# A six-stage decoder kernel: where the products with ones and the division stand in the causal attentions' order

## Chip, cores, metric

The kernel runs on one core of a Trainium2 chip. The metric is the device time of one execution in microseconds, from the first to the last instruction with what lies around them; smaller is better. Times of runs are given as a median with the lowest and highest. A profile is one execution, taken by the hardware profiler.

The engines are named as in the profile: PE is TensorE (PEld its weight loads), DVE VectorE, ACT ScalarE, POOL GpSimd, SP the engine that issues most DMAs. Each runs its own instructions in the order of the program and waits for the others by semaphores.

## What is computed

A decoder of two layers over 8 batches of 256 tokens with 512 features, all in float32. Six stages follow one another, each with its residual and layer norm. Three of them are causal attentions, and the change lies in what these share:

```python
x = _layernorm(x + _L0_attn_ref(x, ...))     # differential attention: 32 query heads of 16
x = _layernorm(x + _L0_xattn_ref(x, ...))    # long convolution
x = _layernorm(x + _L0_ffn_ref(x, ...))      # 8 experts, top 2
x = _layernorm(x + _L1_attn_ref(x, ...))     # self attention: 16 heads of 32
x = _layernorm(x + _L1_xattn_ref(x, ...))    # cross attention
x = _layernorm(x + _L1_ffn_ref(x, ...))      # routed attention: 16 heads, shared keys and values
```

In each of the three, for queries q, keys k and values v of a head:

```python
scores = jnp.einsum('bhqd,bhkd->bhqk', q, k) * scale
scores = jnp.where(causal, scores, ...)
probs = jax.nn.softmax(scores, axis=-1)
out = jnp.einsum('bhqk,bhkd->bhqd', probs, v)
```

The differential attention then takes every second head's output, times a factor lambda, from its neighbour's, and normalizes each head's row by the root of its mean square.

## The kernel before, in words

`causal_attention` is one function, called three times: named "a" (the differential one, 8 units a batch, with a function `gather`), "s" (self attention, 4 units a batch) and "r" (routed, 4 units a batch). A *unit* is four heads of one batch of 256 tokens. There are 64 units in "a" and 32 in each of the others. Units are worked on in *slots*: slot u does the first step for unit u, the second for an earlier unit, the third for one still earlier. With `upb` units a batch, the second step is `wait = upb + 1` slots behind and the third `lag = upb + 2`.

The steps of a unit:

- `maxima(u)`: 12 score products (L1287) into `ps_sc`, a group of four PSUM banks with one buffer only. ScalarE copies them to SBUF (`rows`, L1296; two buffers, in "s" one), GpSimd masks them (L1298), VectorE takes the maxima of the rows (L1307), at the slot's end. At the end of a batch VectorE splits these maxima into three bfloat16 terms (`split`, L1314 to L1321), and in the next slot TensorE turns them (`turn`, L1329).
- `weights(u)`: the scores again, transposed, less the maxima (L1350, L1359), into the same `ps_sc` buffer, so after the copy L1296. ScalarE takes the exponential into `pT` (L1367), which frees `ps_sc` for the next slot's maxima. GpSimd masks it (L1368) and, except in the last batch, adds two of its blocks (L1378), so that the sums below need half the products.
- `products(u)`: weights times values (L1393) into one half of the PSUM tile `ps_pv` (one buffer, in the last batch two), weights times ones (L1403) into the other half. VectorE takes the reciprocal of the sums (L1411), then the quotient: in "s" and "r" by one multiplication (L1417), in "a" by `gather`. The products with values need the mask L1368, those with ones the sum L1378 as well.

`gather` in "a" multiplies by the reciprocal for units of even number in the batch (L438). For odd ones VectorE also multiplies by minus lambda (`second`, L441), and GpSimd adds that to the even one's (L442), in `yT`.

Around these, slots do other work of TensorE, in order of due time: projections for later groups, transposes, output projections (`fill`, by a budget; `need`, what is due). What is to happen later is noted by `at(slots, place, ...)`: at a slot's "start", at its "mid", at its "end", or as work to "fill". `add_norm_later` adds an output to x; GpSimd's reciprocal root (L145, L146) is issued at that slot's "end", and the norm is applied at the next slot's "mid" by VectorE (L160).

`finish` runs after the last unit of a batch. In "a" it notes, among others, ScalarE's Square of all of `yT` at the next slot's "start" (L562), so ahead of that slot's copy L1296 in ScalarE's order, then sums of squares on TensorE (L514) and VectorE's means (L521). In "s" and "r" the output work of the batch is filled in from the next slot on. "s" has at "mid" also VectorE's sums of arriving tokens (L1214), and "r" the spreading of keys (L2145) before they are transposed (L2069).

The order on TensorE, VectorE, ScalarE and GpSimd is the order of the program (`manual_schedule`). A slot before the end of the units runs: maxima, some fill, `sums(u)` (products, with reciprocal and division, and at the end of a batch `finish`), the events at "mid", `weights`, more fill, what is due, the turn, a last fill, the rows' maxima, the events at "end". In the last slots, where no new unit begins, `weights` stand first and `sums` behind them.

## Time and profile before

| | us |
|---|---|
| runs: median (lowest to highest), 3 runs | 2091.62 (2087.61 to 2092.78) |
| profiled execution | 2084.03 |
| its span, first to last instruction | 2082.3 |
| TensorE busy | 1926.0 |
| VectorE busy | 1236.9 |
| GpSimd busy | 851.9 |
| ScalarE busy | 615.3 |
| mean granted TensorE clock | 0.979 |

Busy time of the engines in stretches that lie within the three attentions:

| attention | stretch, us | PE | DVE | ACT | POOL |
|---|---|---|---|---|---|
| "a" | 52 to 445 (393) | 352.30 | 286.69 | 213.43 | 280.83 |
| "s" | 1140 to 1435 (295) | 290.15 | 180.85 | 116.71 | 136.18 |
| "r" | 1880 to 2036 (156) | 136.50 | 131.55 | 82.01 | 105.43 |

How to read the profile: an instruction is given with its line, its engine, what it writes and reads, and the tile's shape. An engine's idle time stands before the instruction that ended it, with what released that instruction. Matmuls overlap, so their busy time is that of the union. One row of the order of time can stand for several instructions alike. Each float32 product appears as two matmuls. An instruction can have waited for several others; the one that came last is named.

Slots are numbered from 0 in each attention and begin with the maxima's first product. In "a" slot 0 begins at 14.62 us and slot 63 at 388.91; in "s" slot 0 at 1101.90; in "r" slot 0 at 1826.90.

### The profile page before, as it was taken

To read this page: it belongs to the slowest core of one execution; us is meant where nothing else is said; L and a number is where in the kernel's file an instruction comes from. 1 tells how busy PE (TensorE), PEld (TensorE's weight loads), DVE (VectorE), ACT (ScalarE), POOL (GpSimd) and SP (SyncE) were. 2 spreads that over 40 slices of the span, in tenths; PEclk is the share of its full clock that TensorE was granted. 3 is DMA by queue.
4 is the path that set the end of the run, shared out by engine and by line. 5 is a ranking of instruction groups with operands and counts; after the bars stand their busy time and mean duration, and the time that the engine had idled before them with its cause. 6 is when DMAs were issued, how large, how long until landed. Compare 5 with 4: busy or idle time off the path is not lost. (4 is left out here: it accounts for less than half of the span.)

```text
span 2082.3 us, 46237 instructions
## 1 busy us (share of the span) xinstructions
PE 1926.0 (92%) x20068; PEld 1122.6 (54%) x20068; DVE 1236.9 (59%) x1879; ACT 615.3 (30%) x787; POOL 851.9 (41%) x945
## 2 busy tenths in 40 slices
PE   7979999879999999999969999998999999988985
PEld 5545555444444446666635545544878778454443
DVE  4677777658889876122225657457343442536887
ACT  4555555520000003211114344431101011235552
POOL 2677777646555834000014545344000000216763
PEclk9999999989999999999989999999999999999997
DMA  6799943326114217223122202002000000170000
GB/s 220 307 399 387 386 139 78 88 69 224 44 58 140 80 51 233 85 72 138 61 86 83 78 31 89 3 2 103 21 21 31 21 31 1 43 233 12 30 24 31
DMA packets 141627, 220.27 MB, mean 106 GB/s; under 512 B 27440, under 2 KB 56240, under 8 KB 141424
## 3 DMA queue, kind: packets, MB, share of 16 engines
q1 hardware_dynamic: 134960, 196.97, 27.5%
q0 software_dynamic: 6464, 20.32, 2.9%
q8 instruction: 160, 2.62, 0.5%
q14 instruction: 43, 0.35, 0.1%
HBM read 106.51 MB, written 123.34 MB: 110 GB/s over the span
## 5 line engine op out<-in xcount | busy, mean ns | idle before, releaser
L1411 DVE RECIPROCAL rsum<-ps_pv 128x256 f32<-128x256 f32 x128 | 224.5, 1754 | 220.2 <-PE ps_pv L1403 220.2
L177 PE MATMUL ps_y<-kv,wt 128*128 128x512 f32 x640 | 280.2, 597 | 5.4 <-POOL kv L607 2.7
L1367 ACT ACTIVATE pT<-ps_k 128x1536 f32<-128x1536 f32 x128 | 185.7, 1451 | 239.1 <-PE ps_k L1359 233.5
L1307 DVE TENSOR_REDUCE neg<-rows 128x12 f32<-128x1536 f32 x128 | 222.9, 1742 | 48.2 <-POOL rows L1298 48.1
L1296 ACT COPY rows<-ps_q 128x1536 f32<-128x1536 f32 x128 | 184.1, 1438 | 154.2 <-PE ps_q L1287 101.1
L1368 POOL TENSOR_SCALAR_AFFINE_SELECT pT<-pT 128x1024 f32<-128x1024 f32 x128 | 140.7, 1100 | 186.2 <-ACT pT L1367 186.1
L177 PEld LDWEIGHTS ps_y<-kv,wt 128*128 128x128 f32 x640 | 120.9, 191 | 156.7 <-issue 137.4
L1298 POOL TENSOR_SCALAR_AFFINE_SELECT rows<-rows 128x1024 f32<-128x1024 f32 x128 | 141.2, 1103 | 154.0 <-ACT rows L1296 153.4
L1378 POOL TENSOR_TENSOR pT<-pT 128x512 f32<-128x512 f32 x112 | 147.1, 1313 | 9.3
L1204 POOL DMA_INDIRECT w_l1x<-ys,slots x32 | 33.5, 1046 | 258.5 <-DMA ys<-y_m 250.9
L207 PE MATMUL ps_f<-xT,w_l1a 128*32 128x256 f32 x2048 | 122.0, 384 | 0.7 <-ACT xT L232 0.7
L145 POOL TENSOR_SCALAR rstd<-bn_mv 128x1 f32<-128x1 f32 x80 | 16.6, 207 | 206.8 <-DVE bn_mv L151 200.5
L1112 PE MATMUL po_m<-dn,hT 128*128 (+1 forms) x216 | 98.7, 594 | 1.0 <-ACT hT L1102 1.0
L1403 PE MATMUL ps_pv<-pT,ones_v 128*32 128x256 f32 (+1 forms) x1152 | 85.2, 378 | 14.7 <-POOL pT L1378 14.6
L645 DVE TENSOR_REDUCE yc<-z 128x64 f32<-128x512 f32 x128 | 86.2, 674 | 5.6 <-POOL w_l1a L646 5.2
L207 PEld LDWEIGHTS ps_f<-xT,w_l1a 128*32 128x32 f32 x2048 | 62.2, 111 | 45.3 <-issue 7.3
L1287 PE MATMUL ps_q<-kz,qT 32*128 32x128 f32 x1536 | 62.2, 292 | 16.8 <-ACT pT L1367 13.4
L1287 PEld LDWEIGHTS ps_q<-kT,qT 32*128 32x128 f32 x1536 | 48.7, 186 | 50.4 <-ACT pT L1367 17.3
L1350 PE MATMUL ps_k<-qT,kT 32*128 32x256 f32 (+1 forms) x1024 | 69.8, 359 | 5.1 <-ACT rows L1296 2.9
L1287 PEld LDWEIGHTS ps_q<-kz,qT 32*128 32x128 f32 x1536 | 49.8, 190 | 45.4 <-ACT pT L1367 31.8
L1091 DVE TENSOR_TENSOR h_b<-h_b,pg 128x352 f32<-128x352 f32 x36 | 18.8, 521 | 92.4 <-ACT h_b L1090 92.4
L1287 PE MATMUL ps_q<-kT,qT 32*128 32x128 f32 x1536 | 61.0, 288 | 13.4 <-ACT pT L1367 8.5
(385 smaller groups left out, 3617.4 us busy)
## 6 DMA issues: line engine op xcount, KB each, us to landing
xs<-zero SPq DMA_DIRECT2D x8, 4352.0 KB, 32.5
ys<-zero SPq DMA_DIRECT2D x8, 4352.0 KB, 33.1
filters<-in_L_xattn_k SPq DMA_DIRECT2D x4, 2560.0 KB
first_h<-xs SPq DMA_DIRECT2D x36, 256.0 KB, 2.7
ys<-y_m SPq DMA_DIRECT2D x36, 256.0 KB, 2.0
gu<-in_L_ffn_gate_up_proj SPq DMA_DIRECT2D x3, 2816.0 KB, 16.4
wt<-filters SPq DMA_DIRECT2D x32, 256.0 KB, 2.6
sorted_x<-zero SPq DMA_DIRECT2D x1, 5120.0 KB, 34.7
```

The lines of the kernel that those rows point to most:

```text
L177: nc.tensor.matmul(ps, lhsT=lhsT(k), rhs=rhs(k), start=(k == 0), stop=(k == n - 1))
L207: nc.tensor.matmul(ps[cs], lhsT=lhsT[:, cs], rhs=rhs, start=start, stop=stop)
L645: nc.vector.tensor_reduce(yc[:, lb], z, AX.X, ALU.add)
L1112: nc.tensor.matmul(po, lhsT=hT[:m, i, :], rhs=dn[i][:m, bass.ds(e, 1), :], start=(i == 0), stop=(i == len(FCH) - 1),)
L1287: nc.tensor.matmul(block[:, s, j, :], lhsT=q(rows, c, b * S + i * P, P), rhs=k(rows, c, b * S + keys * P, P), start=True, stop=True,)
L1296: nc.scalar.copy(d.rearrange("p j s k -> p s j k"), block)
L1298: nc.gpsimd.affine_select(out=rows, in_=rows, compare_op=ALU.is_ge, fill=-FAR, base=0, pattern=[[0, 8], [-1, P]], channel_multiplier=1,)
L1307: return lambda: nc.vector.tensor_reduce(neg[u // upb % 2][:, :, :, c], d, AX.X, ALU.max, negate=True)
L1367: nc.scalar.activation(p[:, 0:3].rearrange("p j s q -> p s j q"), block, AF.Exp)
L1368: nc.gpsimd.affine_select(out=p[:, 0:2].rearrange("p j s q -> p (j s) q"), in_=p[:, 0:2].rearrange("p j s q -> p (j s) q"), compare_op=ALU ...
L1378: nc.gpsimd.tensor_tensor(p[:, 3], p[:, 1], p[:, 2], ALU.add)
L1411: nc.vector.reciprocal(r, ps[:, 1, :])
```

## The change

`products(u)` is cut in two. Its first part allocates the PSUM tile and issues the products with the values. It returns a function, `divided`, that issues the rest: the products with ones, the reciprocal, and the division or `gather`. `sums(u)` returns a function too, which calls `divided` and, at the end of a batch, `finish`. In the slots that begin a unit that function is called behind the events at "mid" and behind `weights`; in the last slots it is called at once.

On TensorE the products with ones thus stand behind the scores for the weights. On VectorE the reciprocal and the division stand behind what is issued at "mid". On GpSimd the addition L442 of `gather` stands behind the mask L1368 and the sum L1378 that `weights` issue. What `finish` notes is noted behind them, for the same later slots. No instruction is added or left out.

```diff
+                def divided():
+                    first = p[:, 0:3:2] if late else p[:, 0:4:3]
+                    for j in range(2 if late else 1):
+                        for s in range(4):
+                            nc.tensor.matmul(
+                                ps[32 * s : 32 * s + 32, 1, j * P :],
+                                lhsT=ones_v,
+                                rhs=p[:, 1, s, :] if j else first[:, :, s, :],
...
+                    r = work.tile([P, S], F32, tag="rsum", name="rsum")
+                    nc.vector.reciprocal(r, ps[:, 1, :])
...
+                return divided
...
             def sums(u):
-                nonlocal per_batch
-                if lag <= u < units + lag:
-                    products(u - lag)
+                if not lag <= u < units + lag:
+                    return lambda: None
+                divided = products(u - lag)
+
+                def rest():
+                    nonlocal per_batch
+                    divided()
                     if (u - lag) % upb == upb - 1:
                         n = (u - lag) // upb
                         per_batch = finish(work, pools, 2 * n, yT.pop(n), at)
+
+                return rest
...
-                    sums(u)
+                    rest = sums(u)
                     happen("mid")
                     if u >= wait:
                         weights(u - wait)
+                    rest()
...
-                    sums(u)
+                    sums(u)()
```

More of the change, by code (lines that the diff above doesn't have):

```diff
@@ L1399, in products @@
                         )
-                first = p[:, 0:3:2] if late else p[:, 0:4:3]
-                for j in range(2 if late else 1):
-                    for s in range(4):
-                        nc.tensor.matmul(
-                            ps[32 * s : 32 * s + 32, 1, j * P :],
-                            lhsT=ones_v,
-                            rhs=p[:, 1, s, :] if j else first[:, :, s, :],
-                            start=(j == 0),
-                            stop=(j == 1 or not late),
-                        )
-                r = work.tile([P, S], F32, tag="rsum", name="rsum")
-                nc.vector.reciprocal(r, ps[:, 1, :])
-                if c == 0:
-                    yT[u // upb] = work.tile([P, KB, S], F32, tag="yT", name="yT_b")
-                if gather:
-                    gather(work, pools, at, yT[u // upb], u // upb, c, ps[:, 0, :], r)
-                else:
-                    nc.vector.tensor_tensor(yT[u // upb][:, c, :], ps[:, 0, :], r, ALU.mult)
+                def divided():
[6 more added lines that the diff above has]
+                                rhs=p[:, 1, s, :] if j else first[:, :, s, :],
+                                start=(j == 0),
+                                stop=(j == 1 or not late),
+                            )
+                    r = work.tile([P, S], F32, tag="rsum", name="rsum")
+                    nc.vector.reciprocal(r, ps[:, 1, :])
+                    if c == 0:
+                        yT[u // upb] = work.tile([P, KB, S], F32, tag="yT", name="yT_b")
+                    if gather:
+                        gather(work, pools, at, yT[u // upb], u // upb, c, ps[:, 0, :], r)
+                    else:
+                        nc.vector.tensor_tensor(yT[u // upb][:, c, :], ps[:, 0, :], r, ALU.mult)
+                return divided
             upg = 2 * upb
```

## The prediction

> **What bounds the kernel now.** I read the table of busy time first, then TensorE's waits over the whole span, then the same waits inside the first attention, then one pair of slots in order of time.

> ```profile
> PE 1926.0 (92%) x20068; PEld 1122.6 (54%) x20068; DVE 1236.9 (59%) x1879; ACT 615.3 (30%) x787; POOL 851.9 (41%) x945
> ```

> TensorE (PE) is busy 92% of the span. Only its idle time, or work of it that other waits hide, can be won. The waits (who, line, waited for: us in total, times, longest) that touch the change:

> ```profile
> PE ps_q L1287 <- ACT pT L1367: 21.9, 18, 1.6
> PE ps_pv L1403 <- POOL pT L1378: 14.6, 34, 0.6
> ...
> PE ps_k L1350 <- ACT rows L1296: 3.8, 10, 0.7
> ```

> and, of these, in the first attention alone (0 to 450 us):

> ```profile
> PE ps_q L1287 <- ACT pT L1367: 13.4, 12, 1.6
> PE ps_pv L1403 <- POOL pT L1378: 11.1, 26, 0.6
> ```

> So the products with ones wait for GpSimd's sum L1378, and the next maxima wait for the exponential L1367 to free the one score buffer. Those two are what the change can win. The scores for the weights hardly wait for the copy L1296 now: 3.8 us. Slots 33 and 34 of the first attention in order of time (start, length, engine, line):

> ```profile
> 198.49 0.95 PE L1287 MATMUL ps_q<-kz,qT 32*128 32x128 f32 x24
> ...
> 199.51 1.44 ACT L1296 COPY rows<-ps_q 128x1536 f32<-128x1536 f32 x1 [1.23 <-PE ps_q L1287]
> ...
> 200.26 0.83 PE L1393 MATMUL ps_pv<-pT,v 128*32 128x256 f32 x16
> ...
> 200.91 0.61 PE L1403 MATMUL ps_pv<-pT,ones_v 128*32 128x256 f32 x8
> ...
> 201.45 0.71 PE L1350 MATMUL ps_k<-qT,kz 32*128 32x256 f32 x8
> 201.59 1.76 DVE L1411 RECIPROCAL rsum<-ps_pv 128x256 f32<-128x256 f32 x1 [0.75 <-PE ps_pv L1403]
> ...
> 202.68 1.45 ACT L1367 ACTIVATE pT<-ps_k 128x1536 f32<-128x1536 f32 x1 [1.73 <-PE ps_k L1359]
> ...
> 203.95 0.73 POOL L442 TENSOR_TENSOR yT_b<-yT_b,second 128x256 f32<-128x256 f32 x1 [1.84 <-DVE quads L505]
> 204.18 0.76 PEld L1287 LDWEIGHTS ps_q<-kz,qT 32*128 32x128 f32 x24 [0.68 <-ACT pT L1367]
> ...
> 204.63 1.09 POOL L1368 TENSOR_SCALAR_AFFINE_SELECT pT<-pT 128x1024 f32<-128x1024 f32 x1
> 204.71 1.06 ACT L562 ACTIVATE w_l<-yT_b 128x1024 f32<-128x1024 f32 x1 [0.58 <-POOL yT_b L442]
> ...
> 205.68 1.42 ACT L1296 COPY rows<-ps_q 128x1536 f32<-128x1536 f32 x1
> ...
> 205.81 1.28 POOL L1378 TENSOR_TENSOR pT<-pT 128x512 f32<-128x512 f32 x1
> ...
> 207.71 0.71 PE L1350 MATMUL ps_k<-qT,kz 32*128 32x256 f32 x8
> ```

> Two distances set a slot. From the maxima to the scores for the weights at least 0.95 + 0.07 + 1.44 + 0.05 = 2.51 us (maxima, handover, copy, handover). From those scores to the next maxima at least 1.10 + 0.12 + 1.45 + 0.05 = 2.72 us (the score group is 1.10 long). Slot 33 has 2.96 and 2.73. Also to be seen: L442 runs ahead of L1368 on GpSimd, which so starts at 204.63 though the exponential ended at 204.13; and the Square L562 stands on ScalarE ahead of slot 34's copy.

> **The change, part by part.** *Eight products with ones move* behind the scores. They last 0.61 us and overlap the product before them by 0.18, so they are worth 0.43. In slot 33 the first distance falls from 2.96 to 2.53, just above 2.51, and the second takes the 0.43: a slot without waits gains nothing. The cover of the copy is gone: what is late on ScalarE in front of it is now late on TensorE.

> *Slots that wait.* Where L1403 waits for the sum (22 times in the inner slots of the first attention), the first distance falls to the 2.51 floor: slot 14, for example, has 2.40 + 0.95 = 3.35, so 3.35 - 2.51 - 0.43 = 0.41. With 0.40 each, 8.8 us. Where the next maxima wait for the exponential, the moved 0.43 hides in that wait; seven such slots away from the heads' turn treated below: 3.0 us. Three slots (29, 35, 59) already stand at the copy's floor and only get the ones added: -1.3 us. Sum: 10.5 us won, of 24.5 waited. Bounds: 0 to 24.5; the floors decide for the middle.

> *GpSimd's order.* In the first attention L442 now stands behind L1368 and L1378 (it was ahead). That helps the sum, and is in the 0.40 above. But once in eight slots the Square reads what L442 wrote, and the next copy stands behind the Square. Slot 33 and 34 anew: scores at 201.02; exponential 202.25 to 203.70; L1368 to 204.84; L1378 from 204.93 to 206.21; L442 to 206.95; Square from 207.00, copy 0.97 behind its start, as now, from 207.97 to 209.39; scores at 209.44, where now they are at 207.71: +1.73, and the ones behind them +0.43, together 2.2 us. The reciprocal is not what is late: 202.73 + 1.76 + 0.03 + 0.49 = 205.01, before 206.2. This happens in slots 18, 26, 34, 42, 50 and 58. By the same working slot 26, where VectorE is late anyhow, pays 1.1, and slot 50, whose forerunner wins nothing, 2.7. Six times 2.2 is +13.2 us (bounds 6.6 and 16.2).

> *VectorE's order.* Reciprocal and division start 1.10 + 0.61 - 0.43 less the old overlap, about 1.15 us, later; the rows' maxima L1307 queue behind them, at the end of a batch the split into terms, and behind that TensorE's turn L1329. In the order of time the turn follows its terms by 0.96, 0.46, 0.90, 0.65, 3.62 and 0.26 us in the first attention's inner turns. VectorE's small copies there took 0.97 to 1.18 us instead of 0.20 where a GpSimd instruction was running, so part of the shift is met by such a pause falling away. I take 2.0 us over three turns (none: 0; the whole shift at five: 5.8). The end of the first and third attention hangs on such a turn (waits 0.79 and 1.92 us): +1.1 each.

> [...]

> *Second attention.* Its TensorE is busy 290.15 of 295 us (1140 to 1435). No waits for the sum. Two slots at the copy's floor: +0.9. Three copies were late because VectorE finished the maxima late (TensorE waits 0.34, 0.68, 0.34); VectorE's norms and sums at "mid" now run in the time in which it waited for the ones, so some two thirds of 1.36 go: -0.9. Net 0.

> *Third attention.* Won: slot 7 of it 0.7 (its products waited 1.47 for the mask, the ones 0.50 for the sum); keys spread at "mid" now stand ahead of the reciprocal, so the waits of 0.65, 1.07 and 1.07 for L2145 shrink, less what the turn behind takes back: 1.55; two exponential waits 0.8. Lost: twice VectorE's two norms (1.95 us for both) stand ahead of the reciprocal where the next product waits for its buffer: 0.7 each; the tail 1.1. Net -0.5.

> No DMA, no instruction is added or removed. SP's queue is passed only at "mid", whose output stores stay where they were, before the scores.

> The switch between groups of 32*128 and 128*32: each costs the overlap of 0.18 less 0.07, 0.11 us. Filled slots have as many as before; ten empty ones get two more, 2.2 us, inside the exponential's wait of up to 1.6: taken at nothing, 2.2 if uncovered. [...]

> **Sum.** First attention -10.5 + 13.2 + 2.0 + 1.1 = +5.8; second 0; third -0.5. Together +5.3 us on the profiled execution, 2084.03 us (span 2082.3 and 1.7 around it): 2089.3. That execution lies 7.6 below the median of the runs, 2091.62, so on their scale I forecast 2097 us.

> **Rivals.** *The late L442 is cheap.* If the Square or the copy behind it is not what slots 18 to 58 wait for, 13.2 goes and the wins stay: -8 us, 2084. For it: 24.5 us of waits lie open. Against: ScalarE's row for L562 shows it starting with L442's end and the copy with its own. Chance 0.17.

> *VectorE's shift is paid everywhere.* In the third attention VectorE is busy 131.55 of 156 us (1880 to 2036). If there the division's end, not TensorE, lets the next product in, from the point where its slack (in quiet slots the next product starts 2.75 us after the reciprocal ends, 0.42 of it the division) is under the 1.15 shift plus the norms that now stand ahead, each of some 12 slots pays 1.0: 2097 + 12 = 2109. Against: quiet slots keep over 1 us. Chance 0.16.

> *The change does nothing to the order,* because TensorE's weight loads run ahead or the balance is exact: 2091.6. The order is written by hand on four engines, so I give 0.05. The forecast keeps 0.62.

> **How the numbers follow.** The forecast's own range is 2092 to 2103 (the bounds 6.6 and 16.2 of the Square, 0 and 5.8 of the turns). With part of both rivals: 2085 to 2107. A measurement here tells 0.3%, 6.3 us: 2085.3 and 2097.9. The forecast lies inside that, with some 0.47 of its weight above 2097.9: slower 0.62 x 0.47 + 0.16 = 0.45; same 0.62 x 0.53 + 0.05 = 0.38; faster 0.17.

> **What would show it.** Right: L1403 no longer waits for L1378; L1350 waits for L1296 far more than 3.8 us, most of it in six places behind L562; L562 waits for L442 over a microsecond where now it is at most 0.6; L1378 ends before L442 starts; L1287's wait for L1367 falls below 21.9. Wrong: if waits for L1296 stay near 4 us, the Square was no matter, and the kernel is faster; if L1393 comes to wait for L1417 or L438 in many slots, VectorE's shift is the cause and the time lies above 2103.

## The result, and the profile after

| | before | after |
|---|---|---|
| runs: median (lowest to highest), us | 2090.57 (2087.61 to 2092.78) | 2116.45 (2116.31 to 2125.73) |
| ratio of times, with its 95% interval | | 1.0138 (1.0120 to 1.0155) |
| profiled execution, us | 2084.03 | 2116.31 |
| its span, us | 2082.3 | 2114.6 |
| mean granted TensorE clock | 0.979 | 0.972 |

The changed kernel is 1.4% slower. The forecast was 2097 us, with a range up to 2107. Slower had the largest of the three chances; the size lay outside the range.

In the changed kernel the product with ones is L1404, the reciprocal L1412, the division L1418; the lines up to L1393 keep their numbers. From the page, the table of busy time and two of the costliest groups (busy time and mean ns of one, idle time before them and its releaser):

```profile
PE 1939.1 (92%) x20068; PEld 1134.9 (54%) x20068; DVE 1227.1 (58%) x1879; ACT 618.4 (29%) x787; POOL 847.6 (40%) x945
...
L1404 PE MATMUL ps_pv<-pT,ones_v 128*32 128x256 f32 (+1 forms) x1152 | 89.3, 393 | 0.0
L1350 PE MATMUL ps_k<-qT,kz 32*128 32x256 f32 (+1 forms) x1024 | 71.0, 364 | 19.6 <-ACT rows L1296 19.3
```

TensorE does the same 20068 products and is busy 13 us longer, at a mean clock of 0.972 in place of 0.979. The products with ones no longer wait for anything (0.0, before 14.7). The scores for the weights now wait for the rows' copy. TensorE's waits over the whole span (us in total, times, longest):

```profile
PE ps_k L1350 <- ACT rows L1296: 26.6, 32, 3.4
...
PE ps_q L1287 <- ACT pT L1367: 11.8, 15, 1.1
PE ps_pv L1393 <- POOL pT L1368: 10.8, 8, 2.8
PE ps_n L1329 <- DVE terms L1318: 8.6, 5, 3.0
PE ps_pv L1393 <- DVE yT_b L1418: 7.6, 6, 2.7
PE ps_ss L514 <- ACT w_l L562: 6.4, 2, 3.4
PE ps_pv L1393 <- POOL rows L1298: 6.2, 2, 3.1
PE pt_ss L527 <- DVE means L521: 5.0, 5, 2.0
...
PE ps_o L207 <- DVE yT_b L559: 4.4, 3, 2.2
...
PE ps_n L1329 <- DVE yT_b L559: 3.2, 1, 3.2
```

L1350's wait went from 3.8 to 26.6 us, L1287's from 21.9 to 11.8, and the 14.6 of L1403 are gone. So both announced wins are there, and the announced loss is larger than both. New in size are L1393's wait for the division L1418 (before 2.7), L514's for the Square (2.5), and L207's and L1329's for VectorE's scaling L559 (0.9 each). The two waits that the profile puts down to GpSimd's mask of the rows, L1298, belong to the division as well: these products don't read the rows, and in both places (slots 116 and 124) the division ended 0.03 to 0.05 us before that mask.

Where the 32.3 us of the two spans lie, worked out from the first product of each slot's maxima in the two traces (from start to start; the first attention up to the start of slot 63):

```
part                                              before    after   difference
before slot 0 of the first attention               14.62    13.66     -1.0
first attention: slots 18, 26, 34, 42, 50, 58      42.18    63.92    +21.7
first attention: slots that became shorter                          -10.9
first attention: other slots that became longer                      +9.9
between first and second attention                712.99   715.62     +2.6
second attention, slot 0 to 31                    295.44   295.37     -0.1
up to slot 1 of the third                         437.44   438.01     +0.6
third attention, slot 1 to 31                     201.15   210.12     +9.0
behind                                             46.39    46.80     +0.4
```

The stretch between the first and the second attention begins with the first attention's slot 63, which has the new order, and its last slots; the long convolution and the experts behind them have no changed code. Its 2.6 us have no explanation here: in the kernels below, some on other chips, it took between 711 and 724.

Slot 34, a batch end, in order of time in the changed kernel (start, length, engine, line; in brackets the idle time before it and what ended it):

```profile
207.04 0.95 PE L1287 MATMUL ps_q<-kz,qT 32*128 32x128 f32 x24
207.68 0.48 DVE L441 SCALAR_TENSOR_TENSOR second<-ps_pv,nlam,rsum 128x256 f32<-128x256 f32 x1
...
208.07 1.32 POOL L1378 TENSOR_TENSOR pT<-pT 128x512 f32<-128x512 f32 x1
...
209.36 0.71 POOL L442 TENSOR_TENSOR yT_b<-yT_b,second 128x256 f32<-128x256 f32 x1
...
210.10 1.06 ACT L562 ACTIVATE w_l<-yT_b 128x1024 f32<-128x1024 f32 x1 [3.28 <-POOL yT_b L442]
...
211.07 1.42 ACT L1296 COPY rows<-ps_q 128x1536 f32<-128x1536 f32 x1
...
212.54 0.71 PE L1350 MATMUL ps_k<-qT,kz 32*128 32x256 f32 x8 [3.33 <-ACT rows L1296]
...
213.57 1.04 PE L1404 MATMUL ps_pv<-pT,ones_v 128*32 128x256 f32 x8
```

The chain is the one predicted: L1378, L442, Square, copy, scores. L441 ended at 208.16 and L1378 at 209.39, so it was GpSimd's order that L442 waited for. The scores start 5.50 us after the slot, forecast as 3.53 + 1.73 = 5.26. What had not been forecast stands in the last line: the eight products with ones take 1.04 us where they took 0.61. In windows of the same slot (length, busy times with their counts, granted clock as the third number from the end):

```profile
210.26:213.68 3.42, 1.14 (x28) 0.87 (x32) 1.62 (x2) 2.23 (x2) 1.74 (x3) 1.00 0.97 377
213.68:217.09 3.41, 3.41 (x36) 1.74 (x39) 2.18 (x2) 1.83 (x2) 1.74 (x2) 0.50 1.04 398
217.09:218.14 1.05, 0.88 (x15) 0.26 (x7) 0.92 (x2) 0.00 (x0) 0.62 (x1) 1.00 1.06 414
```

TensorE is busy 1.14 of 3.42 us, and in the 3.41 us after that its clock is 0.50.

### The profile page after: what moved, and what is told of

Same layout as the page of the kernel before. It is cut to its first block, busy times and chain, and to the rows that moved or that the text cites. A ratio compares the mean times of both kernels' runs of the same rounds, so it can differ in the third digit from the quotient of the medians.

```text
span 2114.6 us, 46249 instructions
## 1 busy us (share of the span) xinstructions
PE 1939.1 (92%) x20068; PEld 1134.9 (54%) x20068; DVE 1227.1 (58%) x1879; ACT 618.4 (29%) x787; POOL 847.6 (40%) x945
## 5 line engine op out<-in xcount | busy, mean ns | idle before, releaser
L1412 DVE RECIPROCAL rsum<-ps_pv 128x256 f32<-128x256 f32 x128 | 224.5, 1754 | 250.0 <-PE ps_pv L1404 250.0
L1307 DVE TENSOR_REDUCE neg<-rows 128x12 f32<-128x1536 f32 x128 | 223.0, 1742 | 48.0 <-POOL rows L1298 47.9
L1367 ACT ACTIVATE pT<-ps_k 128x1536 f32<-128x1536 f32 x128 | 185.7, 1450 | 215.9 <-PE ps_k L1359 213.3
L1296 ACT COPY rows<-ps_q 128x1536 f32<-128x1536 f32 x128 | 184.1, 1438 | 161.2 <-PE ps_q L1287 120.3
L1368 POOL TENSOR_SCALAR_AFFINE_SELECT pT<-pT 128x1024 f32<-128x1024 f32 x128 | 140.8, 1101 | 218.0 <-ACT pT L1367 217.6
L1298 POOL TENSOR_SCALAR_AFFINE_SELECT rows<-rows 128x1024 f32<-128x1024 f32 x128 | 141.1, 1102 | 184.6 <-ACT rows L1296 184.4
L1378 POOL TENSOR_TENSOR pT<-pT 128x512 f32<-128x512 f32 x112 | 144.1, 1287 | 9.3
L207 PE MATMUL ps_f<-xT,w_l1a 128*32 128x256 f32 x2048 | 121.7, 384 | 0.7 <-ACT xT L232 0.7
L1404 PE MATMUL ps_pv<-pT,ones_v 128*32 128x256 f32 (+1 forms) x1152 | 89.3, 393 | 0.0
L1350 PE MATMUL ps_k<-qT,kz 32*128 32x256 f32 (+1 forms) x1024 | 71.0, 364 | 19.6 <-ACT rows L1296 19.3
L207 PEld LDWEIGHTS ps_f<-xT,w_l1a 128*32 128x32 f32 x2048 | 63.9, 111 | 45.6 <-issue 5.0
L1350 PE MATMUL ps_k<-qT,kT 32*128 32x256 f32 (+1 forms) x1024 | 70.8, 364 | 9.0 <-ACT rows L1296 7.2
L1287 PEld LDWEIGHTS ps_q<-kT,qT 32*128 32x128 f32 x1536 | 49.2, 188 | 47.4 <-issue 15.7
L207 PE MATMUL ps_o<-w_l,yT_b 128*32 128x512 f32 x512 | 67.3, 631 | 5.2 <-DVE yT_b L559 4.4
L177 PE MATMUL pg<-gu,xT_b 128*128 x216 | 70.4, 462 | 0.9 <-ACT xT_b L232 0.9
## 6 DMA issues: line engine op xcount, KB each, us to landing
xs<-zero SPq DMA_DIRECT2D x8, 4352.0 KB, 32.3
```

The lines of the kernel that those rows point to most:

```text
L177: nc.tensor.matmul(ps, lhsT=lhsT(k), rhs=rhs(k), start=(k == 0), stop=(k == n - 1))
L207: nc.tensor.matmul(ps[cs], lhsT=lhsT[:, cs], rhs=rhs, start=start, stop=stop)
L1296: nc.scalar.copy(d.rearrange("p j s k -> p s j k"), block)
L1298: nc.gpsimd.affine_select(out=rows, in_=rows, compare_op=ALU.is_ge, fill=-FAR, base=0, pattern=[[0, 8], [-1, P]], channel_multiplier=1,)
L1307: return lambda: nc.vector.tensor_reduce(neg[u // upb % 2][:, :, :, c], d, AX.X, ALU.max, negate=True)
L1350: nc.tensor.matmul(block[:, s, at, :], lhsT=k(rows, c, b * S + j * P, P), rhs=q(rows, c, b * S + j * P, P * (2 - j)), start=True, stop=False,)
```

## The experiments

Theory 1 is the prediction's: in the first attention it is GpSimd's place for L442 that makes the loss, through Square and copy, with the halved clock added, and in the third VectorE's norms ahead of the reciprocal. The rivals are the later reciprocal by itself, or the new place on TensorE. In the expectations the slots are counted through: 64 to 95 are the second attention's, 96 to 127 the third's (108 is the third's slot 12). A ratio is to runs of the kernel before on the same chip.

| kernel | median, us | ratio | 95% |
|---|---|---|---|
| old order at batch ends | 2106.26 | 1.0050 | 1.0033 to 1.0067 |
| GpSimd's order as before | 2126.82 | 1.0146 | 1.0129 to 1.0163 |
| "mid" behind the division | 2140.60 | 1.0211 | 1.0194 to 1.0228 |
| added products in the idle | 2121.00 | 1.0120 | 1.0103 to 1.0137 |
| Square behind the copy | 2107.67 | 1.0050 | 1.0031 to 1.0068 |
| before, L442 alone moved | 2114.50 | 1.0073 | 1.0056 to 1.0090 |
| before, "mid" first | 2106.59 | 1.0028 | 1.0016 to 1.0040 |
| old order at norms and batch ends | 2093.31 | 0.9960 | 0.9947 to 0.9973 |
| before, L442 and Square moved | 2082.87 | 0.9974 | 0.9963 to 0.9985 |
| old order a slot earlier too | 2077.95 | 0.9943 | 0.9927 to 0.9959 |
| that, and Square behind the copy | 2078.55 | 0.9950 | 0.9934 to 0.9967 |

**Old order at batch ends** (of the changed kernel):

```diff
                     rest = sums(u)
+                    early = bool(gather) and u >= lag and (u - lag) % upb == upb - 1
+                    if early:
+                        rest()
                     happen("mid")
...
-                    rest()
+                    if not early:
+                        rest()
```

> The changed kernel, but in the first attention the eight slots that finish a batch keep the old order (products with ones, reciprocal, division and addition ahead of the next unit's scores for the weights); all other slots, and the second and third attention, are as in the change. Theory 1 (the addition L442 now stands behind L1368 and L1378 on GpSimd, so the Square comes late, and with it the rows' copy L1296 and TensorE): the six boundary slots 18, 26, 34, 42, 50, 58 return from a loss of 22.6 us to about nothing, the waits on L1378 won in the quiet slots stay: 2116.5 - 20 = 2096, between 2092 and 2100. Rival (VectorE's later division in every slot costs the first attention its 20 us): only some of it comes back, 2108 to 2116.

From 1.0138 to 1.0050 is 0.0088 of 2090, 18 us, where 20 were expected. In the profiled execution the six slots take 46.82 us, 17.1 less than in the change and still 4.6 more than before, and the first attention is 2.8 us over the kernel before. So most of the first attention's loss sits where a batch ends. Which of the moved things makes it is not told by this.

**L442 alone moved** (in the kernel before; L442 noted for a new place behind `weights`):

```diff
+            if n < B - 1:
+                at(0, "add", lambda: nc.gpsimd.tensor_tensor(y, y, d, ALU.add))
+                return
             nc.gpsimd.tensor_tensor(y, y, d, ALU.add)
-            if n < B - 1:
-                return
...
                         weights(u - wait)
+                    happen("add")
```

> The kernel before with one edit: in the first attention the addition L442 is issued on GpSimd behind the mask L1368 and the addition L1378 of the slot; products with ones, reciprocal and division stay where they were. Theory 1: L442 starts when L1378 ends, 2.9 us after the slot's start in place of -0.2, the Square and the copy follow, the six boundary slots lose 2 to 3 us each and some halved clock on top: 12 to 20 us, ratio 1.006 to 1.010. Rival (L442 is late in the change because the division is late, and the place on GpSimd adds nothing): ratio below 1.003.

The six slots take 59.56 us, 17.4 more than before, and nothing moved on TensorE or VectorE. Slot 34, which begins at 208.39 (lines are one higher here):

```profile
209.58 1.29 POOL L1379 TENSOR_TENSOR pT<-pT 128x512 f32<-128x512 f32 x1
210.82 0.73 POOL L443 TENSOR_TENSOR yT_b<-yT_b,second 128x256 f32<-128x256 f32 x1
...
211.59 1.06 ACT L563 ACTIVATE w_l<-yT_b 128x1024 f32<-128x1024 f32 x1 [3.24 <-POOL yT_b L443]
212.55 1.42 ACT L1297 COPY rows<-ps_q 128x1536 f32<-128x1536 f32 x1
```

The Square waits 3.24 us, as in the change. GpSimd's order alone thus brings a loss of this size in these slots. It also brings part of the win: the other slots of the first attention together are 6.3 us shorter than before. The rival, by which the place on GpSimd adds nothing, falls.

**Square behind the copy** (of the changed kernel; "late" is a new place behind `rest()`):

```diff
-            at(1, "start", lambda: nc.scalar.activation(sq, yT, AF.Square))
-            at(1, "fill", [(0.7, sums)])
+            at(1, "mid", lambda: nc.scalar.activation(sq, yT, AF.Square))
+            at(1, "late", sums)
...
                     rest()
+                    left -= 0.7 * happen("late")
```

> The changed kernel with one move: in the first attention the Square L562 of a finished batch is issued on ScalarE behind the copy of the slot's rows L1296 instead of ahead of it, and its sums at the end of the slot. The addition L442 stays late. Theory 1 (the boundary slots lose because the copy stands behind a Square that waits for L442, TensorE then waits for the copy, and the idle halves the clock): the scores for the weights start some 3 us after the slot's start again, the six slots give back 14 to 19 of their 21.7 us, ratio to before 1.004 to 1.007. Rival (the later reciprocal on VectorE, or the products with ones in their new place, cost these slots): ratio 1.010 or more.

Ratio 1.0050, as expected. L442 is as late as in the change, but nobody on TensorE's path waits for it:

```profile
203.41 1.44 ACT L1296 COPY rows<-ps_q 128x1536 f32<-128x1536 f32 x1 [1.23 <-PE ps_q L1287]
...
204.71 0.72 POOL L442 TENSOR_TENSOR yT_b<-yT_b,second 128x256 f32<-128x256 f32 x1
...
204.90 0.71 PE L1350 MATMUL ps_k<-qT,kz 32*128 32x256 f32 x8 [0.34 <-ACT rows L1296]
...
205.46 1.06 ACT L562 ACTIVATE w_l<-yT_b 128x1024 f32<-128x1024 f32 x1 [0.61 <-POOL yT_b L442]
```

The scores start 2.51 us after slot 34's start at 202.39, and the six slots take 45.37 us in place of 63.92. With this the link from the Square to the copy is shown.

**GpSimd's order as before** (of the changed kernel; `weights` returns its GpSimd part, which is called behind `rest()`):

```diff
-                    if u >= wait:
-                        weights(u - wait)
+                    masked = weights(u - wait) if u >= wait else None
                     rest()
+                    if masked:
+                        masked()
```

> The changed order on TensorE and VectorE in all three attentions, but on GpSimd the addition L442 stands again ahead of the mask L1368 and the addition L1378, as before the change. Theory 1 (it is GpSimd's order alone that costs the boundary slots): the six slots return, about 20 us, less up to 3 us because L1368 can now wait for L442: 2094 to 2101, with the third attention's loss of about 10 us still there. Rival (VectorE's shift, or the TensorE order itself, costs it): 2108 or more.

A miss: 1.0146, no better than the change. The six slots did gain 7.5 us, but the other slots of the first attention lost 11. The longest of TensorE's waits says why:

```profile
PE ps_pv L1396 <- POOL pT L1369: 27.9, 25, 2.6
```

With the products with ones behind the scores, the division and L442 end later, and a mask L1369 that stands behind L442 is then late for the next slot's products with values: 27.9 us, in the change 10.8. In slot 34, L442 ran 1.21 to 1.94 us after the slot's start; in the change 2.32 to 3.03, before the change -0.23 to 0.50. So of the 2.55 us by which the change delays L442 there, GpSimd's place is the last 1.1, and the later division alone would have made 1.4. The order of GpSimd is enough to bring the loss (L442 alone), but taking it back isn't enough to undo it.

**Added products in the idle** (of the changed kernel, 24 more products in slots 34, 42, 50, 58):

```diff
+                if gather and c == 0 and 2 <= u // upb - 1 <= 5:
+                    for _ in range(6):
+                        for s in range(4):
+                            nc.tensor.matmul(
+                                ps[32 * s : 32 * s + 32, 1, :],
+                                lhsT=ones_v,
...
```

> The changed kernel with added work: in the four boundary slots 34, 42, 50, 58 of the first attention 24 further products with ones are issued on TensorE behind the products with values, into the half of the PSUM tile that the real products with ones overwrite later. They fall into the idle of about 3.3 us that the late copy leaves, and take about 24 x 0.16 = 3.8 us. Theory 1 with the clock (an idle of some 3 us halves the granted clock for the 3.4 us after it, which made these slots cost 4.1 us each in place of 2.2): the clock stays up, each slot gains 1.5 to 2.5 us less an overshoot of about 0.5, in all 4 to 7 us faster than the change, 2109 to 2113. Rival (the clock falls for another reason, or it costs nothing here): the same as the change or up to 3 us slower, 2116 to 2120.

With four times 24 products more the kernel is not slower: 1.0120 against 1.0138, though the two intervals overlap, so that the 4 to 7 us expected aren't shown by the times. The slots must decide: 34, 42 and 50 took 10.29, 9.82 and 10.39 us where the change took 11.10, 11.12 and 12.23. In slot 34, up to the scores and from them on:

```profile
205.31:210.83 5.52, 4.76 (x101) 2.93 (x97) 4.74 (x8) 2.38 (x2) 3.71 (x5) 1.00 1.05 406
210.83:215.60 4.77, 3.74 (x67) 2.16 (x67) 3.00 (x4) 1.78 (x2) 3.06 (x3) 1.00 0.95 365
```

The scores still start 5.52 us after the slot, but the clock stays at 1.00 and the second stretch takes 4.77 us, in the change 5.60. By this pair of executions the halved clock cost 0.8, 1.3 and 1.8 us in these three slots. Slot 58, where the change had no halved clock behind the idle, became 0.3 longer, so the four slots together won 3.6 us. (Where the clock is halved also differs between executions of the same code: slot 108 of the third attention, which got no products, took 9.43 us here and 10.74 in the change, with mean clocks of 0.70 and 0.59 behind its scores.) The 4.77 also show a further wait: it was 3.62 before, 0.43 of the growth are the products with ones, and 0.7 are L527, which waits for VectorE's means L521 behind the later reciprocal (1.03 us here, 0.32 before).

**"Mid" behind the division** (of the changed kernel):

```diff
                     rest = sums(u)
-                    happen("mid")
                     if u >= wait:
                         weights(u - wait)
                     rest()
+                    happen("mid")
```

> The changed kernel with one move: what the schedule puts at the middle of a slot (norms, additions, widening copies, Squares) is issued behind the scores for the weights and behind the products with ones, reciprocal and division, no longer ahead of them. Theory 1 (in the third attention slots 108, 116, 124 lose 3.9, 4.0, 2.2 us and 113, 121 1.3 each because two norms stand ahead of the reciprocal on VectorE): the third attention gives back 8 to 10 us, 2106 to 2109 if the first attention stays as it is. In the first attention the later Squares may cost up to 5 us more. Rival (the third attention's loss is the turn or GpSimd's rows, not the norms ahead of the reciprocal): 2114 or more.

A miss in the whole: its ratio is 0.0073 above the change's, 15 us. In the slots it was aimed at it did what was expected: the third attention's slots 108, 112, 113, 116, 120, 121 and 124 took 48.93 us in place of 60.14. But the other slots there lost more than that, and the third attention as a whole took 212.36 us, 2.2 more than in the change. All that stands at "mid" came later, and the second attention, which the change had left alone, took 310.13 us; the other kernels run on that chip took 297.9 to 298.2.

**"Mid" first** (in the kernel before):

```diff
-                    sums(u)
                     happen("mid")
+                    sums(u)
                     if u >= wait:
```

> The kernel before with one edit, in all three attentions: what the schedule puts at the middle of a slot (the norms L160 above all) is issued ahead of the products with values, products with ones, reciprocal and division; these still stand ahead of the next unit's scores for the weights. Theory 1 (norms ahead of the reciprocal on VectorE cost the third attention its 10 us): slots 108, 112, 113, 116, 120, 121, 124 lose together 8 to 14 us, and slots 40, 48, 56 of the first attention up to 3 more: ratio 1.004 to 1.008. Rival (the TensorE order costs it): ratio below 1.002.

The ratio is 1.0028, between the two theories. The same seven slots took 50.84 us, 6.5 more than before and 9.3 less than in the change. So norms ahead of the reciprocal are less than half of the third attention's loss. By exclusion the rest goes with the later products with ones and the reciprocal behind them; the two runs below put both back in chosen slots, together, so they can't tell one from the other. What tells them apart is VectorE's order, shown below.

**Old order at norms and batch ends** (of the changed kernel):

```diff
+            old_order = {
+                "a": (24, 26, 32, 34, 39, 40, 43, 47, 48, 49, 55, 56, 58),
+                "s": (15, 23),
+                "r": (11, 12, 16, 19, 24, 27),
+            }
...
+                    early = u in old_order[name] or (bool(gather) and (u - lag) % upb == upb - 1)
+                    if early:
+                        rest()
                     happen("mid")
...
```

> The changed kernel, but the old order stands in the slots that finish a batch in the first attention, in the slots that have a norm at their middle (first attention 24, 26, 32, 34, 40, 43, 48, 49, 56, 58; second 15, 23; third 11, 12, 16, 19, 24, 27, each counted from its attention's first slot), and in 39, 47, 55 ahead of a turn. Theory 1 (in a quiet slot the change only removes the wait on L1378, 0.4 to 1.7 us; what it costs is in batch ends and norms): the won waits stay, about 7 us in the first, 1 in the second and 5 in the third attention: 13 us faster than before, ratio 0.992 to 0.997. Rival (the change costs something in every slot): ratio 1.000 or more.

Faster than before, 0.9960, as expected. In the first attention the slots other than the six take 322.62 us, 9.5 less than before: the won waits, without the losses around them. But slot 26 took 12.31 us (before 8.51), and 108, 116 and 124 still 9.41, 8.27 and 9.28 (before 6.81, 7.06 and 6.89), so the third attention as a whole, 203.20 us, won nothing against the 201.15 before.

**Old order a slot earlier too:** `"a"` also has 23, `"r"` also 10, 18 and 26.

> The kernel of the run with the old order at norms and batch ends, with the old order also in slot 23 of the first attention and in slots 10, 18, 26 of the third (106, 114, 122 of all). Theory 1 (slots 108, 116, 124 and 26 still lose 2.6, 1.2, 2.4 and 3.8 us against before because the reciprocal of two slots earlier is still late and holds VectorE's residuals, so that the norms run into the next reciprocal): these four give back 7 to 9 us, 0.9 of won waits is given up: ratio 0.991 to 0.994. Rival (something else in those slots): ratio 0.996, as without these slots.

Slot 26 takes 8.52, 108 6.41, 116 7.06, 124 8.16 us. VectorE's order around slot 108 shows why two slots are needed. In the changed kernel (slot 108 starts at 1937.88):

```profile
1931.13 1.76 DVE L1412 RECIPROCAL rsum<-ps_pv 128x256 f32<-128x256 f32 x1 [1.96 <-PE ps_pv L1404]
...
1933.26 0.68 DVE L267 TENSOR_TENSOR res<-ps_y,x 128x512 f32<-128x512 f32 x1
...
1937.98 1.28 DVE L160 TENSOR_SCALAR x<-res,bn_mv,rstd 128x512 f32<-128x512 f32 x1
1939.18 1.74 DVE L1412 RECIPROCAL rsum<-ps_pv 128x256 f32<-128x256 f32 x1
...
1941.53 1.29 PE L1393 MATMUL ps_pv<-pT,v_r 128*32 128x256 f32 x11 [2.70 <-DVE yT_b L1418]
```

in the kernel with the old order at the norms (slot 108 starts at 1926.10):

```profile
1926.03 1.73 DVE L1412 RECIPROCAL rsum<-ps_pv 128x256 f32<-128x256 f32 x1
1927.79 0.42 DVE L1418 TENSOR_TENSOR yT_b<-ps_pv,rsum 128x256 f32<-128x256 f32 x1
1928.13 0.71 DVE L160 TENSOR_SCALAR x<-res,bn_mv,rstd 128x512 f32<-128x512 f32 x1
```

and with the old order one slot earlier as well (slot 108 starts at 1913.41):

```profile
1912.23 1.73 DVE L1412 RECIPROCAL rsum<-ps_pv 128x256 f32<-128x256 f32 x1
1913.99 0.42 DVE L1418 TENSOR_TENSOR yT_b<-ps_pv,rsum 128x256 f32<-128x256 f32 x1
1914.33 0.54 DVE L160 TENSOR_SCALAR x<-res,bn_mv,rstd 128x512 f32<-128x512 f32 x1
```

In the three traces, the reciprocal next to slot 108's start begins 1.30 us after that start, 0.07 before it and 1.18 before it (as in the kernel before). Of the 2.5 us, 1.4 go with the norm L160 (1.28) ahead of it. The other 1.1 come down VectorE's queue from the reciprocal of slot 106 (1931.13): the residuals L267 of slot 107 stand behind it. The median is 0.9943 of before and the best here. That it beats the version without these four slots rests on the profiled executions (9.0 us in the first and third attention together, all of it in these four slots; the two were taken on different chips); the intervals of the two ratios overlap.

**That, and Square behind the copy:** both edits together.

> The kernel of the run before this one, and in the first attention the Square of a finished batch behind the rows' copy on ScalarE, its sums at the end of the slot. Theory 1 (even where L442 is in time, the Square delays the copy by some 0.5 us and TensorE's next scores by up to 1.0): 2 to 5 us more, ratio 0.988 to 0.993. Rival (this cover is not on the path): the same ratio as without it.

The same as without it (0.9950 and 0.9943); the rival holds. Where L442 is in time, the half microsecond by which the copy stands later behind the Square (in the kernel before it starts 1.50 us after slot 34's start, 1.02 after slot 33's) is covered.

**L442 and Square moved** (in the kernel before, the two edits shown above, TensorE's order untouched):

> The kernel before with two edits in the first attention, and nothing moved on TensorE or VectorE: the addition L442 is issued on GpSimd behind the mask L1368 and the addition L1378 of the slot, and the Square of a finished batch on ScalarE behind the rows' copy, its sums at the end of the slot. Theory 1 (GpSimd's order alone makes both the change's gain, the waits on L1378, and, through the Square, its loss in the boundary slots; the place of the products with ones on TensorE makes neither): the quiet slots win 0.4 to 1.1 us as in the change, the boundary slots are no longer than before, 6 to 10 us faster than before, ratio 0.995 to 0.998. Rival (the waits on L1378 are won by the place of the products with ones): ratio 0.999 or more.

Faster than before, 0.9974 (0.9963 to 0.9985). The six slots take 41.78 us (before 42.18), slots 14, 36 and 52 took 5.83, 5.86 and 6.24 (before 6.25, 6.32 and 6.69). The time won, some 5 us, is a little less than the 6 to 10 expected. Of the 3.9 us between the profiled executions 2.1 lie in the first attention. The third, whose code is the same as before, is 3.3 us shorter (197.86; 200.69 in L442 alone, 201.15 before): a difference of 3 us there, in a single execution, shows nothing. So a part of what the change was to win is had without moving a product, by putting L442 behind L1378, if the Square is taken out of the copy's way; how much, the ratio tells better than the slots.

## Why the prediction was wrong

It came to +5.3 us; the profiled executions differ by 32.3, the medians by 25.9 (before's profiled execution is 6.5 below its median). The terms below are read from those two executions and so add up to some 6 us too much; which of them that touches isn't known. By the steps of the working:

- **Slots that wait, -10.5 us:** 11.8 won and 1.3 lost at the copy's floor; measured 10.9 won, and slots 29 and 35 lost 1.0. Right, with some luck in the number: 1.7 of the 10.9 are slot 61, which had a granted clock of 0.50 before (375.55 to 378.96 us) and not after, and slots 11, 12, 38 and 55, which had such waits, won nothing. Slot 14, forecast 0.41, won 0.41. L1404 waits for nothing, L1287's waits fell to 11.8 us.
- **GpSimd's order, "six times 2.2 is +13.2":** the place and the chain were right, and shown by three runs (old order at batch ends, L442 alone, Square behind the copy). The term was mis-sized: 21.7 us, above its upper bound of 16.2. The delay of the scores was nearly as told: over the six slots they start 11.3 us later after the slot's start, forecast 6 x 1.73 = 10.4. The stretch behind them, from the scores to the next slot, grew by 10.4 us, where 6 x 0.43 = 2.6 had been put down. Slot 34 lost 3.95 us: 1.97 from the later copy (forecast 1.73), 0.43 from the products with ones (as forecast), 0.7 from L527 behind means that stand behind the later reciprocal, and 0.8 from the halved clock. The last two were not in the working. "The reciprocal is not what is late" held for L442, but not for what else stands behind the reciprocal.
- **VectorE's order, 2.0 us over three turns:** the turn slots 40, 48 and 56 lost 1.99, 2.65 and 1.08, together 5.7, just within the bound of 5.8; the value taken was too low. In slot 48 the product that waits is the output's L207, for the scaling L559 that now stands behind the later reciprocal, and a halved clock comes on top (0.50 from 305.83 to 309.25 us). The other longer slots make 4.2 us: 1.0 are the two at the floor, and slot 21's 1.28 is again a stretch at half clock (0.50 from 124.93 to 128.34 us).
- **The pause of VectorE's small copies,** which was to meet part of its shift: of the recorded small instructions of the splits in the first attention 12 of 48 took over 0.5 us before, 8 of 48 after. Before, GpSimd was running for over nine tenths of the length of all 12, but also for more than half of the length of 17 of the other 36.
- **Second attention, 0:** -0.06.
- **Third attention, -0.5:** measured +9.0. The wins were there, and larger than forecast (slots 100, 103, 106, 111, 119 and 126: -5.6, forecast -3.05). The seven slots behind norms lost 15.8 where two times 0.7 had been put down. The prediction looked at the norms ahead of one reciprocal, and not at the queue that the reciprocal before it pushes along; the two together make TensorE wait 2.7 to 3.1 us in three places (slots 108, 116, 124), and each is followed by 6.8 us or more at a granted clock of 0.50.
- **The switch of groups,** taken at nothing, 2.2 us if uncovered: not seen. Slots 31 and 45 have six such changes in place of five and are 0.05 us longer; slots 19, 20, 59 and 60 have two more each and became shorter, by 0.48, 0.69, 0.24 and 1.10 us.
- **The rival "VectorE's shift is paid everywhere" (2109)** came nearer in time, but not as it was told: it is paid in seven slots of 31 of the third attention and in some slots of the first, not in twelve at 1.0 each. Its sign, L1393 waiting for the division, was there in eight places, 13.8 us with the two waits put down to L1298.
- **The range 2092 to 2103** doesn't follow from the bounds that are named for it: 2097 - 6.6 - 2.0 is 2088, and 2097 + 3.0 + 3.8 is 2104.

So three terms of the sum failed. In "six times 2.2 is +13.2" the 2.2 held the late copy and the products with ones alone: what else waits behind the later reciprocal and the halved clock behind the idle time were taken at nothing (10.4 us behind the scores in place of 2.6). The 2.0 for the turns were 5.7. In the third attention, -0.5 against +9.0, not only a size was off: two norms ahead of one reciprocal were priced, and the path by which an earlier reciprocal delays VectorE's residuals and norms, and these the next reciprocal, was missing (losses of 15.8 us, forecast 1.4 and 1.1 for the tail). The clock after an idle time was in none of the three.

## What to carry to other kernels

When an instruction is moved back on one engine, follow every in-order queue that its result feeds for two steps of the loop, not one: here the loss came through GpSimd to ScalarE to TensorE, and through VectorE's reciprocal of two slots earlier. The waits were won here by moving what they waited for (L442 behind L1378, with the Square behind the copy), or by moving the products only where no norm and no batch end is near, and not by moving them in all slots alike. And a new idle time of TensorE is to be priced with the slower clock that was found behind it here: 0.50 for 3.41 us or a multiple of it, which in slots 34, 42 and 50 cost 0.8, 1.3 and 1.8 us.

## What the hardware showed that was not expected

```
idle in a window of 3.41 us    next at full clock    next halved
below 1.4                             7209                 0
1.4 to 1.6                              90                 4
1.6 to 1.8                              44                25
1.8 to 2.0                              18                34
above 2.0                                0               161
```

(Idle is what no product's record covers; windows ahead of TensorE's first product aside. The few records that a trace lacks make it too long in some rows, and windows at a row's border can fall on either side.) So these windows did not have to be idle throughout: of those idle for 1.6 to 1.8 us, about half of 3.41, 25 of 69 were followed by a halved one, of those idle for over 2.0 us (59%) all 161. Whether some 2 to 3 us of waiting halved the clock went with where they fell on the grid. In the change, slot 58 waited 2.19 us for the copy, which the grid cut into windows idle for 0.66 and 1.53 us, and kept its clock; slot 42 waited 2.49, of which 2.42 lay in one window, and lost it (0.50 from 268.29 to 271.70 us).
